# Loading shifted rows for a depthwise convolution by groups of channels to 128 partitions, adding its tiles by transfers, and reordering ScalarE's last instructions

## The chip, the core and the metric

The kernel runs on one core of a Trainium2 chip. The time is the device time of one execution, in microseconds (us). The kernel before takes 2873.85 us (median of three runs, 2868.29 to 2874.54).

## What is computed

Input x has shape [16, 384, 32, 32] in float32: 16 images, 384 channels, 1024 pixels each.

```python
# layer 0: group norm, attention over pixels (8 heads of 48), projection, residual
x = x + proj(softmax(q k^T * 48**-0.5) v)(_gn(x))
# layer 1: group norm, depthwise 7x7 convolution, residual
w_sym = (w + rot90(w, 1) + rot90(w, 2) + rot90(w, 3)) * 0.25
x = x + depthwise_conv(_gn(x), w_sym, padding=3)
```

The kernel exploits that w_sym is symmetric under rotation by 180 degrees only through sums and differences of columns; that part is not touched here.

## The kernel before

**Main body.** The channels lie on the 128 partitions, in three blocks k = 0, 1, 2. For each image b, TensorE makes q, k and v, then for each pair of heads the scores (L518) and the weighted sum (L538), then the projection (L599). ScalarE does the exponentials (L526). VectorE does the convolution of the image before: a tile (b, k) is one block of channels of one image. Its "folding" (fold_ops, L724) is a list of some 40 instructions: sums and differences of columns ("side", L733), multiply-adds into rows ("rows_e", "rows_o" and the output, L736), and adds of shifted rows (L746). ScalarE prepares it: fold_x writes the normalised tile with a margin ("padded", L704), and fold_first the first product of three rows_e tiles (L715). The finished tile is stored by conv_end (L821).

**The end.** Three tiles, PE_TILES = (14, 2), (15, 2) and (15, 1), are convolved by TensorE; of the last image VectorE folds only (15, 0). The route of a tile on TensorE is:

1. conv_begin normalises the tile and conv_store (L893) writes it to a DRAM buffer "xd": one channel takes 2 planes (rows of the image with even and with odd number) of PLANE = 19 rows of 32.
2. conv_load (L904) reads it back as "sh", one tile of 128 partitions by 4 groups by 512 for each half a of the channels. On the partitions lie 16 channels times RI = 8 shifts in the vertical; each of the 4 groups has another 16 channels. Before, there is one transfer for each shift i, to the 16 partitions from 16·i on, with 4 rows of 2 KB each: 8 transfers of 128 KB for a load. At the end (late["tail"]), odd i are issued by ScalarE's queue, the others by SP's.
3. conv_on_pe (L926) multiplies with banded matrices ("mat", made by conv_matrices from weights "wsh" and a stack of identities "eye"); a piece for one half has 28 matmuls: 7 horizontal taps times 4 groups. The tap dx is the outer loop, so the first 4 matmuls read all 4 groups.
4. conv_take (L953): ScalarE copies the half from PSUM to "rows". conv_perm (L958): TensorE sorts even and odd rows with a permutation into "ps_rows".
5. conv_add (L978): VectorE adds ps_rows to the residual x1 (L980), and a transfer stores the result (L981).

**What sets the order.** The schedule is written by hand: each engine runs its instructions in the order in which the Python program issues them. A planner estimates times: `clock` for TensorE, `vclock` for VectorE. `after(wait, cost, f)` queues a piece of VectorE work that becomes due `wait` us from now; `catch_up` issues due work first and otherwise the next instruction of the folding (`tap`); `applies` is a queue of ScalarE work. fast_end (L1461) issues the end of the last image: the statistics, the start of the convolutions, ScalarE's fold_x and fold_first, and the first permutation. The last loop of `run` issues the pieces on TensorE; between the first two pieces of (15, 2) on TensorE stands the matmul of the check of the softmax sums (check_tensor, L1373, L1376); it gives VectorE two tiny instructions (L1378, L1379), whose place on VectorE depends on what the planner has issued by then.

Transfers issued by SP or ScalarE use eight completion semaphores in turn; a transfer that takes one waits until the transfer that had it eight places before has landed. An engine that issues a transfer is held by that wait.

Of the kernel before, what the change touches and what calls it, by code (L numbers as in the profile page):

```python
# [10 lines left out]
F32 = mybir.dt.float32  # L11
I32 = mybir.dt.int32
AF = mybir.ActivationFunctionType
ALU = mybir.AluOpType
AX = mybir.AxisListType

P = 128
# [28 lines left out]
def kernel(  # L46
# [25 lines left out]
    nc = tc.nc  # L72

    B, C, H, W = x.shape
    N = H * W
# [4 lines left out]
    HALF = N // 2  # L80
# [39 lines left out]
    def run(general):  # L120
        tag = "g" if general else "f"
        with ExitStack() as stack:
# [14 lines left out]
            tpool = pool("tpool", 2)  # L137
# [6 lines left out]
            def psum(name):  # L144
                return ps_s.tile([P, 2, HALF], F32, tag="s", name=name)

            xns, x1s, qks, os_, accs, es, xn1s = {}, {}, {}, {}, {}, {}, {}
            xds, shs, pss, mats, psums = {}, {}, {}, {}, {}
# [32 lines left out]
            late, pps = {}, {}  # L181
# [18 lines left out]
            ident = wpool.tile([P, P], F32, name="ident")  # L200
# [13 lines left out]
            wsh = wpool.tile([P, 2, 8, 2, KS], F32, name="wsh")  # L214
# [446 lines left out]
            def by_rows(t):  # L661

                return t.rearrange("p (m q w) -> p q m w", q=2, w=W)

            def grids(t):
                return t.rearrange("p q (m w) -> p q m w", w=W)
# [153 lines left out]

            def conv_end(b, k):  # L821

                (nc.scalar if b == B - 1 and not general else nc.gpsimd).dma_start(  # L823
                    out[b, k * P : (k + 1) * P].rearrange("p h w -> p (h w)"), x1s.pop((b, k))
                )

# [5 lines left out]
            RI, CG = KS + 1, P // (KS + 1)  # L832
            NG = P // CG
            PLANE = (H // 2 + PAD) * W

            def conv_prepare():

                w_d = dconv.tile([C, (KS + 2) * KS], F32, tag="w", name="w_d")
                zero = tpool.tile([P, N], F32, tag="t", name="zero")[:, 0 : 2 * W]
                nc.gpsimd.memset(zero, 0.0)  # L840
                w_rows = w_d.rearrange("(k p) t -> p k t", p=P)
                with nc.allow_non_contiguous_dma(reason="small, once"):
                    nc.gpsimd.dma_start(
                        w_rows[:, :, KS : (KS + 1) * KS], wsym.rearrange("p k i j -> p k (i j)")
                    )
                    none = zero[:, 0 : NK * KS].rearrange("p (k t) -> p k t", k=NK)
                    nc.gpsimd.dma_start(w_rows[:, :, 0:KS], none)
                    nc.gpsimd.dma_start(w_rows[:, :, (KS + 1) * KS :], none)
                    for n, k in enumerate(PE_K):
                        for i in range(RI):  # L850
                            nc.gpsimd.dma_start(
                                wsh[CG * i : CG * (i + 1), n].rearrange("p g t d -> p g (t d)"),
                                bass.AP(
                                    w_d.tensor,
                                    w_d.offset + (k * P * (KS + 2) + i) * KS,
                                    [[(KS + 2) * KS, CG], [CG * (KS + 2) * KS, NG], [1, 2 * KS]],
                                ),
                            )
                for bk in PE_TILES:
                    xd = dconv.tile([P, 2 * PLANE], F32, tag=f"x_{len(xds)}", name=f"xd_{len(xds)}")  # L860
                    xds[bk] = xd

                    for lo, n in ((0, 1), (H // 2 + 1, 2), (H // 2 + 3, 2), (2 * PLANE // W - 1, 1)):
                        nc.gpsimd.dma_start(xd[:, lo * W : (lo + n) * W], zero[:, 0 : n * W])
                for q in range(RI):
                    src = ident[:, CG * q : CG * (q + 1)]
                    if q == 0:
                        nc.gpsimd.tensor_copy(eye, src)
                    else:
                        nc.gpsimd.tensor_tensor(eye, eye, src, ALU.add)  # L870
                for row in range(2):
                    nc.gpsimd.tensor_copy(
                        perm[:, row].rearrange("p (g c) -> p g c", c=CG),
                        ident.rearrange("p (g t c) -> p t g c", t=2, c=CG)[:, 1 - row],
                    )
# [28 lines left out]
            def conv_load(b, k, a):  # L904

                t = qkpool.tile([P, 2, N], F32, tag="qk", name=f"sh_{b}_{k}_{a}")
                t = t.rearrange("p a n -> p (a n)").rearrange("p (g n) -> p g n", n=HALF)
                xd = xds[b, k]
                for i in range(RI):
                    (nc.scalar if late.get("tail") and i % 2 else nc.sync).dma_start(  # L910
                        t[CG * i : CG * (i + 1)],
                        bass.AP(
                            xd.tensor,
                            xd.offset
                            + a * NG // 2 * CG * 2 * PLANE
                            + (0 if i % 2 else PLANE)
                            + i // 2 * W,
                            [[2 * PLANE, CG], [CG * 2 * PLANE, NG // 2], [1, HALF]],
                        ),
                    )  # L920
                shs[b, k, a] = t
# [29 lines left out]
            perms = deque()  # L951

            def conv_take(b, k, a):  # L953
                if a == 0 or (b, k) not in shs:
                    shs[b, k] = epool.tile([P, 2, HALF], F32, tag="e", name=f"rows_{b}_{k}")
                nc.scalar.copy(shs[b, k][:, a, :], pss.pop((b, k, a)))

            def conv_perm(b, k, a):  # L958

                nonlocal clock  # L960
                if (b, k) not in pss:
                    pss[b, k] = psum(f"ps_rows_{b}_{k}")
                part = slice(64 * a, 64 * a + 64)
                for row in range(2):
                    nc.tensor.matmul(
                        pss[b, k][part, row, :],
                        lhsT=perm[:, row],
                        rhs=shs[b, k][:, a, :],
                        start=True,
                        stop=True,  # L970
                    )
                clock += 2.2
                if (b, k) == PE_TILES[-1]:
                    after(0.5, 1.3, lambda: conv_add(b, k, part, (nc.scalar, nc.sync)[a]))
                elif a == 1:
                    after(3.5 if b < B - 1 else 0.5, 1.3, lambda: conv_add(b, k, slice(0, P), nc.gpsimd))

            def conv_add(b, k, part, queue):  # L978
                dst = by_rows(x1s[b, k][part])
                nc.vector.tensor_tensor(dst, grids(pss[b, k][part]), dst, ALU.add)  # L980
                queue.dma_start(  # L981
                    out[b, k * P + part.start : k * P + part.stop].rearrange("p h w -> p (h w)"),
                    x1s[b, k][part],
                )
# [89 lines left out]
            clock, vclock, catching = 0.0, 0.0, False  # L1074
# [10 lines left out]
            def after(wait, cost, f):  # L1085

                nonlocal count
                count += 1
                heapq.heappush(later, (now() + wait, count, cost, f))

            applies, count_a = [], 0
# [292 lines left out]
            def loads(n):  # L1384
                while n and pe_loads and pe_loads[0][0] in xn1s:
                    (b, k), a = pe_loads.popleft()
                    conv_load(b, k, a)
                    n -= 1
# [15 lines left out]
            def conv_rows():  # L1404
                for p in perms:
                    conv_take(*p)
                while perms:
                    conv_perm(*perms.popleft())
# [52 lines left out]
            def fast_end(b):  # L1461
                nonlocal clock, vclock
                assert not applies
                x1_stats[b].groups_on_pe(late["masks"], tap, lambda: conv_piece(False))
                conv_piece(False)
                x1_chains(b, x1_stats[b])
                clock = now()
                vclock = clock + 1.0
                after(0.0, 1.2, check_vector)
                heapq.heappop(applies)[-1]()  # L1470
                loads(2)
                clock += 3.0
                heapq.heappop(applies)[-1]()
                conv_rows()
                clock += 4.5

            def once(key, when):
                if when and key not in late:
# [4 lines left out]
            for b, n0, size in [  # L1483
# [31 lines left out]
                if b == B - 1:  # L1515
# [10 lines left out]
                    if once("ones", r >= 32):  # L1526
                        t = wv.rearrange("p k c -> p (k c)")[:, 0:N]
# [15 lines left out]
            while later or state["done"] < len(order) or active or pe_conv or perms:  # L1543
# [6 lines left out]
                else:  # L1550
                    clock = now() + 1.0
# [53 lines left out]
```

## Time and profile before

| | us |
|---|---|
| median of three runs | 2873.85 |
| the profiled execution | 2872.72 |
| its span (first to last instruction) | 2870.9 |
| TensorE busy | 2832.4 |
| VectorE busy | 2083.9 |
| ScalarE busy | 1649.1 |
| GpSimd (POOL) busy | 250.6 |
| last store issued | 2865.20 |

The granted TensorE clock is 0.994 of full speed. A line of a timeline gives start, length, engine, line of the source, operation, output <- inputs, and in brackets how long the engine stood idle before and who released it. SPq and ACTq are transfer issues on SP's and ScalarE's queues; the length there is the time over which a group of issues was spread. A "landing stamp" is an increment of the completion semaphore of a transfer, as the trace records it. TensorE's busy time is modelled; the last instruction of VectorE's folding ends at 2865.17.

### The profile page before, as it was taken

Reading aid. Unit: us, or ns where it says so; the run is one execution under the profiler, and the core shown is the slowest. Engines: PE = TensorE matmul, PEld = TensorE weight load, DVE = VectorE, ACT = ScalarE, POOL = GpSimd, SP = SyncE. Lnnn points to the kernel's source line nnn. Section 1 sums busy time; section 2 is a strip of 40 time slices with the busy share of each in tenths; the row PEclk is TensorE's granted clock in tenths of the full one; section 3 lists DMA queues with packets and bytes.
Section 4 is the critical chain, followed back from the end, with each engine's and each line's share of the span. In section 5 each row is a group of like instructions: output and inputs, shape, how many; then the busy total and the mean of one; then the engine's idle time right before and its main releaser. Section 6 shows DMA issues by size and latency. Waiting matters only on the chain.

```text
span 2870.9 us, 46047 instructions
## 1 busy us (share of the span) xinstructions
PE 2832.4 (99%) x19342; PEld 1115.2 (39%) x19342; DVE 2083.9 (73%) x2257; ACT 1649.1 (57%) x1925; POOL 250.6 (9%) x410
## 2 busy tenths in 40 slices
PE   9999999999999999999999999999999999999995
PEld 5344343433434344343433434344343433434331
DVE  4502968959597695968959597695968959597776
ACT  2637647475674747647475674747647375674730
POOL 3201012210101001010010101001010010101000
PEclk9999999999999999999999999999999999999998
DMA  6612131211212112130211212112130211212215
GB/s 239 189 37 49 32 75 29 53 49 44 63 33 62 45 37 64 32 75 24 50 50 44 63 33 62 45 37 63 32 75 24 50 50 44 64 33 60 78 39 103
DMA packets 75657, 167.35 MB, mean 58 GB/s; under 512 B 31952, under 2 KB 34000, under 8 KB 73904
## 3 DMA queue, kind: packets, MB, share of 16 engines
q0 software_dynamic: 32400, 107.53, 14.3%
q1 hardware_dynamic: 41536, 54.16, 7.5%
q10 hardware_dynamic: 1504, 2.62, 0.6%
q8 instruction: 154, 2.52, 0.4%
q14 instruction: 63, 0.52, 0.1%
HBM read 117.09 MB, written 28.68 MB: 51 GB/s over the span
## 4 chain that ended last, share of the span: by engine, by line
PE 95%; DVE 3%; DMA 1%; issue 1%; ACT 0%; ACTq 0%; POOL 0%; SPq 0%; DVEq 0%; POOLq 0%
PE ps_s L518 30%; PE acc L538 30%; PE ps_qk L447 17%; PE ps_v L473 9%; PE ps_proj L599 8%; DVE x L746 1%; DVE rows_e L736 1%; DMA sh<-xd 1%; PE warm L1325 0%; DVE side L733 0%; DMA inv<-rec 0%; DMA inv<-inv 0%; DVE rows_o L736 0%; DVE x L736 0%; DVE x L980 0%
## 5 line engine op out<-in xcount | busy, mean ns | idle before, releaser
L526 ACT ACTIVATE e<-ps_s 128x1024 f32<-128x1024 f32 x1024 | 1021.2, 1030 | 448.1 <-PE ps_s L518 447.4
L538 PE MATMUL acc<-e,v 64*64 64x512 f32 x8192 | 1040.5, 588 | 0.6 <-ACT o L551 0.6
L518 PE MATMUL ps_s<-qk 48*64 48x512 f32 x8192 | 1040.8, 589 | 0.0
L733 DVE TENSOR_TENSOR side<-padded 128x1024 f32<-128x1024 f32 x270 | 329.0, 1219 | 345.5 <-ACT padded L704 345.5
L736 DVE SCALAR_TENSOR_TENSOR rows_e<-side,even,rows_e 128x1024 f32<-128x1024 f32 x405 | 509.6, 1274 | 85.6 <-ACT rows_e L715 84.0
L538 PEld LDWEIGHTS acc<-e,v 64*64 64x64 f32 x8192 | 308.8, 132 | 575.8 <-issue 574.2
L518 PEld LDWEIGHTS ps_s<-qk 48*64 48x64 f32 x8192 | 307.5, 132 | 577.4 <-issue 525.8
L447 PE MATMUL ps_qk<-x,wqk 128*128 128x512 f32 x1152 | 502.8, 595 | 0.0
L447 PEld LDWEIGHTS ps_qk<-x,wqk 128*128 128x128 f32 x1152 | 218.2, 191 | 278.0 <-issue 272.4
L746 DVE TENSOR_TENSOR x<-x,rows_o 128x992 f32<-128x992 f32 (+3 forms) x271 | 309.8, 1144 | 3.0
L746 DVE TENSOR_TENSOR x<-x,rows_e 128x992 f32<-128x992 f32 (+2 forms) x270 | 310.8, 1151 | 0.0
L454 ACT COPY qk<-ps_qk 128x1024 f32<-128x1024 f32 x96 | 97.2, 1012 | 319.4 <-PE ps_qk L447 319.4
L473 PE MATMUL ps_v<-wv,x 128*128 128x384 f32 x768 | 252.6, 486 | 0.0
L599 PE MATMUL ps_proj<-o,wp 128*128 128x512 f32 x540 | 234.2, 592 | 0.0
L493 ACT COPY v<-ps_v 64x384 f32<-64x384 f32 x256 | 121.4, 474 | 122.5 <-PE ps_v L473 120.0
L473 PEld LDWEIGHTS ps_v<-wv,x 128*128 128x128 f32 x768 | 145.9, 190 | 108.2 <-issue 14.3
L736 DVE SCALAR_TENSOR_TENSOR rows_o<-side,odd,rows_o 128x1024 f32<-128x1024 f32 x135 | 172.8, 1280 | 1.6
L736 DVE SCALAR_TENSOR_TENSOR x<-side,even,x 128x1024 f32<-128x1024 f32 x135 | 172.5, 1278 | 0.0
L823 POOL DMA_DIRECT2D out<-x x44 | 24.8, 563 | 1600.3 <-DVE x L746 1599.8
L715 ACT ACTIVATE rows_e<-padded,even 128x1024 f32<-128x1024 f32 x135 | 146.7, 1166 | 11.0 <-DMA sh<-xd 11.0
L599 PEld LDWEIGHTS ps_proj<-o,wp 128*128 128x128 f32 x540 | 102.6, 190 | 126.2 <-issue 117.4
L607 ACT ACTIVATE x<-ps_proj,bp 128x1024 f32<-128x1024 f32 x45 | 50.1, 1114 | 167.6 <-PE ps_proj L599 167.6
(145 smaller groups left out, 1013.1 us busy)
## 6 DMA issues: line engine op xcount, KB each, us to landing
x<-in_x POOLq DMA_DIRECT2D x90, 512.0 KB, 5.5
inv<-inv SPq DMA_DIRECT2D x126, 256.0 KB
out<-x POOLq DMA_DIRECT2D x46, 512.0 KB, 3.0
xs<-in_x POOLq DMA_DIRECT2D x42, 512.0 KB, 6.4
qk<-qk POOLq DMA_DIRECT2D x96, 128.0 KB, 4.1
o<-o SPq DMA_DIRECT2D x180, 32.0 KB
sh<-xd SPq DMA_DIRECT2D x32, 128.0 KB
x<-in_x SPq DMA_DIRECT2D x6, 512.0 KB
```

The lines of the kernel that those rows point to most:

```text
L447: nc.tensor.matmul(ps[:, h, :], lhsT=wqk[:, k, s, t, :], rhs=xns[b][:, k, h * HALF : (h + 1) * HALF], start=(k == 0), stop=(k == NK - 1),)
L454: nc.scalar.copy(halves(qks[u][:, s, :]), ps)
L473: nc.tensor.matmul(ps[:, j, 0:C], lhsT=xns[b][:, k, t * P : (t + 1) * P], rhs=wv[:, k, :], start=(k == 0), stop=(k == NK - 1),)
L493: nc.scalar.copy(dst[:, :, 0 : HEADS // 2 * (D + 1)].rearrange("p k (h d) -> p k h d", d=D + 1)[:, :, :, 0:D], src.rearrange("p k (h d) -> ...
L518: nc.tensor.matmul(ps[64 * c : 64 * c + 64, a, :], lhsT=qk[r, 1, 64 * kb : 64 * kb + 64], rhs=qk[r, 0, h * HALF : (h + 1) * HALF], start=True,
L526: nc.scalar.activation(es[n], ps, AF.Exp, scale=SCALE)
L538: nc.tensor.matmul(accs[a][64 * j : 64 * j + 64, :], lhsT=v[rows, kb, c : c + 64], rhs=e[rows, j, :], start=(kb == 0), stop=(kb == 2 * NT ...
L599: nc.tensor.matmul(ps[:, h, :], lhsT=wp[:, t, o * P : (o + 1) * P], rhs=os_[b, t // 2][:, t % 2, h * HALF : (h + 1) * HALF], start=(t == 0 ...
L715: nc.scalar.activation(grid(rows_e[dy - 1]), padded_view(i), AF.Identity, scale=even[:, k, dy, 0:1],)
L733: vec.tensor_tensor(grid(sides[n]), padded_view(i, j), padded_view(i, -j), op)
L736: vec.scalar_tensor_tensor(dst, src, w, dst, ALU.mult, ALU.add)
L746: vec.tensor_tensor(dst, dst, src[:, lo + dy * W : hi + dy * W], op)
```

## The change

- conv_load issues 4 transfers of 256 KB for a load, one for each group of 16 channels, each to all 128 partitions, all on SP's queue. The partitions are now sorted by pair of shifts (4), then channel, then parity of the row, so that source and destination can be walked together: the source pattern is [W, 4], [PLANE, 32], [1, 512]. The new function `inputs(i)` gives the partitions of shift i, every second of 32; the weights and the stack of identities follow it.
- For (14, 2) and (15, 2), ScalarE copies ps_rows from PSUM to a tile "t", GpSimd's queue adds it to x1 by an accumulating transfer, and conv_end stores x1, on GpSimd's queue too. Before, VectorE added and GpSimd's queue stored. (15, 1) keeps VectorE's add, in two halves; its due time is 6.0 us after the permutation instead of 0.5.
- fast_end: ScalarE's copies of (14, 2) go ahead of fold_first, and the permutation goes behind it. The planner's clock grows by 3.0 at another place and no longer by 4.5 at the end.
- By the new clocks, the order on VectorE changes where the diff doesn't show it. The two reductions of the check (L1378, L1379 before) came after the first five instructions of the folding of (15, 0) and after the add of (14, 2); they now come before all of them. On TensorE the order is as before.

```diff
             def conv_end(b, k):

-                (nc.scalar if b == B - 1 and not general else nc.gpsimd).dma_start(
+                nc.gpsimd.dma_start(
                     out[b, k * P : (k + 1) * P].rearrange("p h w -> p (h w)"), x1s.pop((b, k))
                 )
...
+            def inputs(i):
+
+                first = i // 2 * 2 * CG + 1 - i % 2
+                return slice(first, first + 2 * CG - 1, 2)
...
-                                wsh[CG * i : CG * (i + 1), n].rearrange("p g t d -> p g (t d)"),
+                                wsh[inputs(i), n].rearrange("p g t d -> p g (t d)"),
...
-                    src = ident[:, CG * q : CG * (q + 1)]
+                    src = ident[:, inputs(q)]
...
-                for i in range(RI):
-                    (nc.scalar if late.get("tail") and i % 2 else nc.sync).dma_start(
-                        t[CG * i : CG * (i + 1)],
+
+                for i in range(NG // 2):
+                    nc.sync.dma_start(
+                        t[:, i],
                         bass.AP(
                             xd.tensor,
-                            xd.offset
-                            + a * NG // 2 * CG * 2 * PLANE
-                            + (0 if i % 2 else PLANE)
-                            + i // 2 * W,
-                            [[2 * PLANE, CG], [CG * 2 * PLANE, NG // 2], [1, HALF]],
+                            xd.offset + (a * NG // 2 + i) * CG * 2 * PLANE,
+                            [[W, RI // 2], [PLANE, 2 * CG], [1, HALF]],
                         ),
                     )
...
                 if (b, k) == PE_TILES[-1]:
-                    after(0.5, 1.3, lambda: conv_add(b, k, part, (nc.scalar, nc.sync)[a]))
+                    after(6.0, 1.3, lambda: conv_add(b, k, part, (nc.scalar, nc.sync)[a]))
                 elif a == 1:
-                    after(3.5 if b < B - 1 else 0.5, 1.3, lambda: conv_add(b, k, slice(0, P), nc.gpsimd))
+                    t = tpool.tile([P, N], F32, tag="t", name=f"conv_{b}_{k}")
+                    nc.scalar.copy(by_rows(t), grids(pss.pop((b, k))))
+                    nc.gpsimd.dma_start(x1s[b, k], t, accum_op=ALU.add)
+                    conv_end(b, k)
...
                 loads(2)
+                for p in perms:
+                    conv_take(*p)
+                heapq.heappop(applies)[-1]()
+                while perms:
+                    conv_perm(*perms.popleft())
                 clock += 3.0
-                heapq.heappop(applies)[-1]()
-                conv_rows()
-                clock += 4.5
```

## Prediction

> **What bounds the kernel now.** I read the table of slices first: TensorE is busy in every slice but the last, which reads 5. The body is therefore bound by TensorE's attention matmuls, and every line of the diff that runs more than once runs after 2700 us of the 2870.9 us span (the weight rows of conv_prepare run once, near 500 us, and are hidden). So only the last 170 us matter. Second I asked for the chain that ended last, from 2700 us on (start, length, what).
>
> ```profile
> 2798.11 2.83 DMA xd<-xn
> 2802.47 7.83 DMA sh<-xd
> 2810.69 3.23 ACT rows_e L715 x3
> 2814.53 4.08 PE ps_rows L965 x8
> 2818.63 1.23 DVE x L980
> 2819.86 1.13 DVE side L733
> ...
> 2843.51 1.13 DVE x L980
> ...
> 2853.25 1.23 DVE x L980
> ...
> 2863.98 1.20 DVE x L746 x2
> ```
>
> Read downwards: the normalised rows are stored, shifted rows are loaded, ScalarE gets to rows_e, TensorE permutes the tile (14,2), VectorE adds it, and from then on VectorE works without a gap to 2865.2. VectorE idled 19.5 us before 2818.63. Third, the timeline of the same stretch says why (start, length, engine or queue, line).
>
> ```profile
> 2801.09 22.32 SPq L910 DMA_DIRECT2D sh<-xd  x16
> 2801.12 9.52 ACTq L910 DMA_DIRECT2D sh<-xd  x8
> ...
> 2818.53 6.12 PE L941 MATMUL ps_conv<-sh,mat 128*32 128x512 f32 x56
> ...
> 2824.47 0.17 PE L1376 MATMUL ps_again<-lim,ones 128*1 128x2 f32 x1
> ...
> 2825.57 0.14 DVE L1378 TENSOR_REDUCE good<-ps_again 1x1 f32<-1x2 f32 x1
> ...
> 2849.26 1.93 PE L965 MATMUL ps_rows<-rows,perm 128*64 128x512 f32 x4 [0.70 <-ACT rows L956]
> ```
>
> Eight load issues in ScalarE's stream hold it for 9.5 us (each waits for the completion semaphore of an earlier transfer), so rows_e, the two copies and the permutation come late. VectorE's add L980 stands before its folding, so the folding waits too. Fourth, the windows give the loads' rate (us, PE, PEld, DVE, ACT, POOL busy; clock; DMA share; GB/s).
>
> ```profile
> 2799.00:2801.00 2.00, 1.05 (x12) 0.13 (x4) 0.12 (x2) 0.66 (x1) 0.00 (x0) 1.00 0.99 376
> 2819.00:2827.00 8.00, 7.33 (x74) 1.96 (x66) 7.97 (x9) 0.58 (x1) 0.59 (x1) 1.00 1.06 134
> ```
>
> The store to DRAM over 128 partitions moves 376 GB/s; the loads of 16 partitions each move about 131 (landing stamps: one transfer of 128 KB per 1.0 us from 2804.2 to 2835.5). All engines are equally full in both.
>
> [...] The new load's destination begins with 128 partitions, but its source begins with the 4 shifts ([W, 4], [PLANE, 32], [1, 512]), so **it would run on 4 engines**. The trace shows the rule at work once: sum<-o, whose sides both begin with 2, lands with three stamps (2711.57 at once, then 2712.25 and 2712.29), where the 16-partition loads land with sixteen. The forecast goes by this rule. I found no transfer in the trace whose two sides begin with unequal numbers.
>
> **The price of the load.** On one engine a 2 KB packet takes 82 ns at the least, and at 376 to 392 GB/s sixteen engines do 24 GB/s each. Four engines give at most 98 GB/s: 10.7 us for one load of 1 MB (four transfers). [...] I take the middle, **82 GB/s, 12.8 us**, against 8.0 us now, and keep both ends.
>
> **The sum, part by part**, against the profiled execution (2872.72 us; the median shown, 2873.85, lies 1.1 higher, and I add that at the end).
>
> 1. *ScalarE's end.* The 16 load issues leave its stream (15.3 us of it). After padded (2799.7) come the two copies (0.56, 0.58, once the convolution of (14,2) ends at 2800.05) and rows_e (3.2), done at 2804.5 instead of 2813.9; the permutation of (14,2) ends near 2805. What is late next: the order of VectorE's instructions has changed. The reduction L1378 now stands before all the folding. It waits for the matmul L1376, which TensorE reaches only after the first piece of (15,2), 6.1 us long, which waits for the first load. Behind it wait all of VectorE's folding and the two last adds.
> 2. *First load.* Data begin at 2802.7; 12.8 + 0.4 for landing gives 2815.9, the piece ends at 2822.0, and VectorE starts 1.3 later, at 2823.3 (in before, the reduction ran 0.9 behind its matmul and took 0.3 with the next). Its folding began at 2819.8 before.
> 3. *Adds by transfer.* VectorE loses two adds (1.23, 1.22); its work from start to end, 46.5 us, becomes 43.8 with the 0.25 of the check ahead of it. ScalarE gains two copies from PSUM of 128x1024 (1.01 each by L454), POOL two accumulating transfers (0.55 to issue; 5.5 to land by the x loads, 3.0 for the store behind). For (15,2) this ends by about 2859, before the end: hidden. The copy also stands before the copy of (15,1)'s first half, hidden while TensorE waits for the last load; with that cover gone it would cost up to 1 us of TensorE, not of VectorE.
> 4. *Last load.* Four loads in one queue end at 2802.7 + 51.2 + 0.4 = 2854.3. Then the first matmuls of the last piece 1.4 (of 1.85), permutation of the first half 2.0, rest of the piece 4.3, copy 0.65, second permutation 1.95 (the last row above), wake-up and add 1.5: 2866.1. Of VectorE's folding, 10.0 us stand behind this add (10.7 less one L739 that moves ahead). **End 2876.1 instead of 2865.2: +10.9.** VectorE alone would have been done at 2823.3 + 43.8 = 2867.1, so the load decides.
> 5. *Earlier loads, of (14,2).* They share SP's queue with the softmax sums. At 82 GB/s the first ends at 2730.8 (2728.8 now) and inv<-rec behind it as late; the second is issued after inv<-inv, ends at 2747.9, and sum<-o (two engines[...]) behind it. The reciprocal L568 would run at 2749.9 instead of 2748.2: +1.7, of which 0.3 to 0.6 is slack before TensorE's sums at 2774: **+1.4**. At 98 GB/s nothing, at 66 +7.4.
> 6. *Fewer issues on SP (24 less in all), the later due time of the last add (6.0 us), the new channel order, conv_end's queue:* nothing. SP has no other work there but the sums; the last add waits for TensorE anyway; the channel order changes which rows are taken, not how many.
>
> 2872.7 + 10.9 + 1.4 = 2885.0; with 1.1, **2886**. At 98 GB/s step 4 gives +2.5: 2876. At 66 it gives +23.3, with step 5 +30.7: 2904. Break-even is 104 GB/s.
>
> **Rivals.**
> - *All sixteen engines carry the load*[...]: 1 MB in 3.0 us at 350 GB/s. First load 2806.1, VectorE starts at 2813.5, needs 43.8, ends at 2857.3: -7.9; inv<-rec comes earlier, but only the 0.6 of slack before 2774 can be had. **2865, faster.** For it: 376 GB/s of the 128-partition store. Against: the rule and the three stamps. It decides from 104 GB/s upward.
> - *Four engines[...]:* 98 GB/s, **2876**, no change that can be measured. For it: many packets of inv<-inv, 64 partitions on 16 engines, take the minimum of 159 ns for 4 KB. Against: that is over within 16 KB an engine, and the second such transfer is slower.
> - *The rate stays at 131 GB/s* (the change doesn't widen the path): VectorE starts at 2818.5, ends at 2862.3: -2.9, **2871**, no change.
>
> **How the numbers follow.** About 0.2% (5.7 us) is what a measurement of this kernel can tell from no change. Four engines with conflicts: 0.60, 2886 (2880 to 2904). Four engines near their full rate: 0.15. Rate unchanged: 0.04. Sixteen engines: 0.21, 2865. Leaving the fast case out would leave out 0.21, so the range goes from 2863 to 2904. Faster 0.21, no change 0.19, slower 0.60.
>
> **What would show it.** A load landing with 5 stamps and not 16; transfers of 256 KB 2.7 to 4.0 us apart; DMA share near a quarter in the tail; rows_e near 2801 to 2805; L1378's counterpart on VectorE at about 2823 with no folding before it; VectorE idle before each add of (15,1); the last load landing near 2854. If loads land about 0.75 us apart and VectorE begins near 2813, the rule does not hold here and the kernel is faster.

## The result, and the profile after

The changed kernel takes 2886.25 us (median of five runs, 2885.32 to 2887.18), the kernel before 2873.37 us (five runs): a ratio of 1.0051, 95% interval 1.0036 to 1.0066. It is slower by half a per cent, clear of the noise. The forecast was 2886 us, slower. The profiled execution took 2886.04 us, its span 2884.3.

Up to about 2797 us the two kernels run alike, bound by TensorE; the loss lies behind that. The chain that ended last, in the changed kernel (start, length, what):

```profile
2797.40 2.84 DMA xd<-xn
...
2836.18 14.23 DMA sh<-xd
2850.46 1.83 PE ps_conv L944 x9
2852.28 1.86 PE ps_rows L968 x4
2854.14 4.24 PE ps_conv L944 x40
...
2859.04 1.95 PE ps_rows L968 x4
2861.01 1.22 DVE x L986
...
2867.08 1.24 DVE x L986
...
2877.14 1.19 DVE x L746 x2
```

Before, the chain left the loads at 2810.3, went over ScalarE's rows_e and TensorE's permutation, and was VectorE's own work from 2818.6 on. Now the loads hold it until 2850.5, then come the last piece, its permutation, and 17.3 us of VectorE. The timeline of the same stretch:

```profile
2800.14 2.33 PE L968 MATMUL ps_rows<-rows,perm 128*64 128x512 f32 x8 [0.80 <-ACT rows L959]
2800.32 38.42 SPq L916 DMA_DIRECT2D sh<-xd  x16
2800.36 3.25 ACT L715 ACTIVATE rows_e<-padded,even 128x1024 f32<-128x1024 f32 x3
...
2804.81 0.91 POOL L981 DMA_DIRECT2D x<-conv  x1 [8.48 <-ACT conv L980]
...
2814.20 0.55 POOL L823 DMA_DIRECT2D out<-x  x1 [8.48 <-DMA x<-conv]
2814.53 1.92 PE L944 MATMUL ps_conv<-sh,mat 128*32 128x512 f32 x2 [3.13 <-DMA sh<-xd]
2817.20 7.32 PE L944 MATMUL ps_conv<-sh,mat 128*32 128x512 f32 x48 [0.75 <-DMA sh<-xd]
...
2825.38 0.15 DVE L1384 TENSOR_REDUCE good<-ps_again 1x1 f32<-1x2 f32 x1 [26.97 <-PE ps_conv L944]
```

ScalarE is free at once (rows_e ends at 2803.6, before at 2813.9). But the check's reduction, first in VectorE's order, waits until 2825.4 for TensorE, and TensorE for the loads. (The profile counts 56 matmuls for a piece where the program issues 28.) VectorE's waits (total, times, longest):

```profile
DVE good L1384 <- PE ps_conv L944: 27.0, 1, 27.0
DVE x L986 <- PE ps_rows L968: 8.6, 1, 8.6
```

The windows of the load (the clock, the DMA share and GB/s are the last three columns):

```profile
2810.00:2814.00 4.00, 1.40 (x2) 0.00 (x0) 0.00 (x0) 0.00 (x0) 0.00 (x0) 0.50 0.26 69
...
2818.00:2822.00 4.00, 4.00 (x28) 1.53 (x24) 0.00 (x0) 0.00 (x0) 0.00 (x0) 0.54 0.26 101
...
2835.00:2840.00 5.00, 5.00 (x50) 1.44 (x47) 4.96 (x6) 0.58 (x1) 0.00 (x0) 1.00 0.26 98
```

The DMA share is a quarter (0.26): as much as four of sixteen engines, and 98 GB/s. Each transfer lands with five stamps, one at once and four together; a later one has 2826.13, 2826.19, 2826.30 and 2826.37, the next 2.7 us later. A packet of 2 KB takes 87 ns (median), where the loads of before took 236 on one queue and 244 on the other.

### The profile page after: what moved, and what is told of

It is laid out like the page before. It is cut to its first block, busy times and chain, and to the rows that moved or that the text cites. A ratio compares the mean times of both kernels' runs of the same rounds, so it can differ in the third digit from the quotient of the medians.

```text
span 2884.3 us, 45997 instructions
## 1 busy us (share of the span) xinstructions
PE 2843.2 (99%) x19342; PEld 1123.7 (39%) x19342; DVE 2081.3 (72%) x2255; ACT 1650.7 (57%) x1927; POOL 253.3 (9%) x412
```

## Experiments

**How the runs are compared.** Whole runs of one kernel spread by some 8 to 12 us (before: 2868.6 to 2877.1 in thirty runs, 2867.8 to 2879.4 in thirteen others). In the traces, the attention part is alike to a few hundredths, but sits up to 3.4 us earlier or 0.8 later than in the trace of before, by differences in the first 280 us; and in five traces TensorE's clock dropped near 2792, in four for 3.4 us and in one for 10.2 us (windows there show 0.50 to 0.82), which put the tail about 1.6 to 2.3 us later (ScalarE's wait for the statistics is 8.8 or 9.5 us in these and 7.2 in the others). So beside the medians I use the **tail**: from the start of xn's normalisation on VectorE (L363 in the changed kernel, 2796.56 there, 2797.27 before) to the end of the span. "Folding from" and "last load" count from the same point, all three in us.

| kernel | median us | ratio to before, 95% | tail | folding from | last load |
|---|---|---|---|---|---|
| before | 2872.4 to 2874.4 | | 73.7 | 22.5 | 38 |
| changed | 2886.25 | 1.0051 (1.0036 to 1.0066) | 87.7 | 29.1 | 54 |
| dimensions exchanged | 2867.07 | 0.9979 (0.9972 to 0.9986) | 66.7 | 16.8 | 22 |
| late adds | 2878.61 | 1.0025 (1.0012 to 1.0038) | 79.4 | 28.9 | 54 |
| no accumulating transfer | 2883.89 | 1.0040 (1.0026 to 1.0054) | 83.4 | 25.5 | 50 |
| before, new loads | 2878.87 | 1.0021 (1.0010 to 1.0032) | 79.7 | 9.8 | 51 |
| before, all loads on SP | 2867.55 | 0.9975 (0.9965 to 0.9985) | 67.1 | 9.8 | 33 |
| early check | 2881.35 | 1.0024 (1.0014 to 1.0034) | 82.1 | 6.3 | 54 |
| early check, late adds | 2874.03 | 1.0002 (0.9993 to 1.0011) | 74.5 | 6.3 | 54 |
| due time put back | 2886.43 | 1.0044 (1.0028 to 1.0061) | 86.6 | 28.9 | 54 |
| halved transfers | 2957.45 | 1.0289 (1.0272 to 1.0306) | 135.8 | 40 | 99 |
| all three repaired | 2858.70 | 0.9945 (0.9929 to 0.9962) | 56.9 | 6.3 | 22 |

### The dimensions of the source exchanged

```diff
-                first = i // 2 * 2 * CG + 1 - i % 2
-                return slice(first, first + 2 * CG - 1, 2)
+                first = i // 2 + RI // 2 * (1 - i % 2)
+                return slice(first, first + RI * (CG - 1) + 1, RI)
...
-                            [[W, RI // 2], [PLANE, 2 * CG], [1, HALF]],
+                            [[PLANE, 2 * CG], [W, RI // 2], [1, HALF]],
```

> The changed kernel with one edit: the two outer dimensions of the load's source change places (channel planes first, shifts second), and the partitions are numbered to match. Bytes, packets, queue, number of transfers and every instruction on the engines stay. Theory A (the outermost dimension of the source, 4, limits the load to 4 engines): landing stamps become 16 or so, 256 KB about 0.75 us apart instead of 2.65, the first four have landed near 2806, VectorE starts near 2813 instead of 2825.4, and the kernel takes about 2865 us. Rival (the load is slow because its rows overlap in DRAM, or because of its bytes, whatever the order): still 2.65 us per 256 KB and 2886 us.

Measured: 2867.07 us. Every transfer lands with sixteen stamps. From 2816.6 to 2820.6 the transfers of 256 KB end 0.63 to 0.69 us apart; before that, while GpSimd's accumulating transfer is under way (it lands at 2816.35), 0.6 to 2.4 us apart. A window, and two lines of the timeline of this kernel:

```profile
2814.00:2820.00 6.00, 5.33 (x36) 1.50 (x28) 4.01 (x6) 0.58 (x1) 0.55 (x1) 1.00 1.04 371
```

```profile
2803.19 12.41 SPq L916 DMA_DIRECT2D sh<-xd  x16
...
2815.95 0.15 DVE L1384 TENSOR_REDUCE good<-ps_again 1x1 f32<-1x2 f32 x1 [14.67 <-PE ps_conv L944]
```

The core's transfers run at 371 GB/s instead of 98, with a DMA share of 1.04 instead of 0.26 (GpSimd's two transfers have a part in this window; by the landings just named, the loads alone reach some 390). The bytes and packets of the loads are the same. The order of two dimensions decided here; the rival (bytes, overlapping rows) falls. VectorE folds from 16.8 instead of 29.1, and then needs the 44 us that the forecast gave it. The change as it stands loses 21.0 us of tail by this alone, and would have been faster than before without it.

### A dose: two engines

```diff
-                for i in range(NG // 2):
+                for i, j in [(i, j) for i in range(NG // 2) for j in range(2)]:
                     nc.sync.dma_start(
-                        t[:, i],
+                        t[P // 2 * j : P // 2 * (j + 1), i],
...
-                            xd.offset + (a * NG // 2 + i) * CG * 2 * PLANE,
-                            [[W, RI // 2], [PLANE, 2 * CG], [1, HALF]],
+                            xd.offset + (a * NG // 2 + i) * CG * 2 * PLANE + 2 * j * W,
+                            [[W, RI // 4], [PLANE, 2 * CG], [1, HALF]],
```

> A dose: the changed kernel with each load transfer cut in two, one for each two pairs of shifts, to 64 partitions each, so that the source begins with a dimension of 2 instead of 4. Theory A (the outermost dimension of the source sets the number of engines): 3 stamps for each transfer, 2 engines, 128 KB per 2.7 us, that is 49 GB/s; 16 transfers for one tile pair of loads more, the last load lands some 40 us later (near 2890), and the kernel takes 2920 to 2930 us. Rival 1 (the number of engines goes by partitions or by packets of a transfer): 5 stamps or more and 2886 us or a little more. Rival 2 (two transfers in a row take different engines): 98 GB/s and 2886 us.

Measured: 2957.45 us. A window and a wait of this kernel:

```profile
2840.00:2860.00 20.00, 10.50 (x58) 2.50 (x56) 1.35 (x3) 0.00 (x0) 0.00 (x0) 0.64 0.13 49
```

```profile
PE ps_proj_last L643 <- DVE o L580: 19.5, 1, 19.5
```

Three stamps each, 128 KB per 2.7 us, 49 GB/s, a DMA share of an eighth (0.13): as theory A says for an outermost dimension of 2. The time I had forecast was some 30 us too low. The wait shows most of that: the earlier loads, those of (14,2), share SP's queue with the softmax sums, and at 49 GB/s TensorE stood still for 19.5 us before L643. That is the forecast's step 5, which I left out of this expectation. The table has most of the rest: the last load lands 45 us later than in the changed kernel where I had said 40, and 37 us stand behind it instead of 34.

### The adds of (15,1): late, and as before

Late adds:

```diff
-                    after(6.0, 1.3, lambda: conv_add(b, k, part, (nc.scalar, nc.sync)[a]))
+                    after(40.0, 1.3, lambda: conv_add(b, k, part, (nc.scalar, nc.sync)[a]))
```

> The changed kernel with the due time of the two adds of (15,1) at 40 us instead of 6, so that they come behind nearly all of VectorE's folding. Theory (VectorE's 8.6 us of idle before the first of these adds lie on the path that sets the end): the folding behind them fills that idle time, the last add still waits for TensorE (second permutation 2861.0), and the end moves from 2878.3 to about 2870: 2878 us, -8.5. Rival (the order on VectorE makes no difference, since the last load sets the end): 2886 us.

Measured: 2878.61 us, tail -8.3. The timeline of VectorE shows both adds at the very end, without a wait:

```profile
2863.40 3.54 DVE L746 TENSOR_TENSOR x<-x,rows_o 128x960 f32<-128x960 f32 x4
2866.86 2.47 DVE L986 TENSOR_TENSOR x<-ps_rows,x 64x1024 f32<-64x1024 f32 x2
```

The 8.6 us of idle time lay on the path. Due time put back:

```diff
-                    after(6.0, 1.3, lambda: conv_add(b, k, part, (nc.scalar, nc.sync)[a]))
+                    after(0.5, 1.3, lambda: conv_add(b, k, part, (nc.scalar, nc.sync)[a]))
```

> The changed kernel with the due time of the two adds of (15,1) put back to 0.5 us. The first add then stands six instructions earlier on VectorE, and before the second one. Theory A (an add of the first half waits wherever it stands, since the load is late): VectorE reaches it near 2847 and waits for the first permutation (near 2854.2), folds 5.6 us, and takes the second add right behind the second permutation at 2861; 16 us follow as before, end near 2877.2 instead of 2878.3: 2885 us, -1. Rival (the later due time by itself carries the 8.6 us of idle time): -6 to -8, 2878 to 2880 us.

Measured: 2886.43 us, tail -1.1. VectorE's two adds in this kernel:

```profile
2852.22 1.22 DVE L986 TENSOR_TENSOR x<-ps_rows,x 64x1024 f32<-64x1024 f32 x1 [7.56 <-PE ps_rows L968]
...
2859.05 1.23 DVE L986 TENSOR_TENSOR x<-ps_rows,x 64x1024 f32<-64x1024 f32 x1
```

The idle time only moved forward to the first add. The second add now stands where the first stood in the changed kernel, and starts at the same moment (2859.05; this trace lies 2.0 us earlier, and there it was 2861.01). Behind that moment there is one add less, 16.1 us of work instead of 17.3. So the later due time by itself costs 1.1 us. What matters is how much of the folding stands behind the adds when the load comes so late.

### The accumulating transfer and store of (14,2) left out

```diff
-                    nc.gpsimd.dma_start(x1s[b, k], t, accum_op=ALU.add)
-                    conv_end(b, k)
+                    if b == B - 1:
+                        nc.gpsimd.dma_start(x1s[b, k], t, accum_op=ALU.add)
+                        conv_end(b, k)
```

> The changed kernel without the accumulating transfer and the store of tile (14,2): that tile is left out of the output, ScalarE's copy of it stays. Theory (the accumulating transfer and the store take turns with the loads on the four engines that carry them, and cost the first load some 5 us): transfers of the first load land 2.65 us apart without the gap, the last of the four near 2812.5 instead of 2817.2, all later ones as much earlier, and the kernel takes about 2881 us, -4.5 to -5. Rival (the gap has another cause, such as the waits for completion semaphores on SP's queue): gap and time stay, 2886 us.

Measured: the four transfers of the first load let TensorE go on at even distances (timeline of TensorE):

```profile
2808.08 1.04 PE L944 MATMUL ps_conv<-sh,mat 128*32 128x512 f32 x2 [3.54 <-DMA sh<-xd]
2810.76 1.91 PE L944 MATMUL ps_conv<-sh,mat 128*32 128x512 f32 x2 [1.63 <-DMA sh<-xd]
2813.44 1.92 PE L944 MATMUL ps_conv<-sh,mat 128*32 128x512 f32 x2 [0.77 <-DMA sh<-xd]
2816.11 6.87 PE L944 MATMUL ps_conv<-sh,mat 128*32 128x512 f32 x48 [0.75 <-DMA sh<-xd]
```

In the changed kernel they start at 2805.72, 2809.49, 2814.53 and 2817.20. The gaps of 3.8 and 5.0 us are gone, the last load lands 4.3 us earlier after xn, the tail is 4.3 us shorter. The medians alone could not show this: 2883.89 against 2886.25, and the intervals of the ratios overlap. In the changed kernel the transfer's stamps show the same from the other side: twelve at 2809.3 to 2809.6, four only at 2813.7 to 2813.9.

### The kernel before with the new loads alone

```diff
-                for i in range(RI):
-                    (nc.scalar if late.get("tail") and i % 2 else nc.sync).dma_start(
-                        t[CG * i : CG * (i + 1)],
+                for i in range(NG // 2):
+                    nc.sync.dma_start(
+                        t[:, i],
```

With it go the source's pattern, `inputs` and its two uses, as in the change; the adds and fast_end stay as before.

> The kernel before with the new loads alone (four engines, all on SP's queue, partitions renumbered); adds, their due times and the order on ScalarE and VectorE stay. Theory (the loads' rate costs, and the freed ScalarE gives back): ScalarE is done with its rows near 2804, VectorE folds from about 2808 on, the last load lands near 2846 to 2850, the last permutation ends near 2857 to 2861 and what stands behind the last add follows: 2874 to 2880 us, slower than before by 1 to 7. Rival (the new loads cost nothing, the loss comes from the adds' new order): 2866 us or less, since VectorE would start 10 us earlier.

Measured: 2878.87 us, tail +6.0 against before. VectorE in this kernel:

```profile
2806.18 1.22 DVE L733 TENSOR_TENSOR side<-padded 128x1024 f32<-128x1024 f32 x1
...
2824.40 0.15 DVE L1380 TENSOR_REDUCE good<-ps_again 1x1 f32<-1x2 f32 x1 [12.34 <-PE ps_conv L943]
...
2858.42 1.23 DVE L982 TENSOR_TENSOR x<-ps_rows,x 64x1024 f32<-64x1024 f32 x1 [0.32 <-PE ps_rows L967]
```

VectorE starts 12.7 us earlier than before, then waits for the check and for the late load. So the loads alone make the kernel slower; the rest of the change adds 8.0 us of tail.

### The kernel before with all its loads on SP's queue

```diff
-                    (nc.scalar if late.get("tail") and i % 2 else nc.sync).dma_start(
+                    nc.sync.dma_start(
```

> The kernel before with one edit: all its loads of 16 partitions go to SP's queue, none to ScalarE's. Theory (the issues in ScalarE's stream hold rows_e and the permutation, and with them VectorE): rows_e done near 2804 instead of 2813.9, VectorE's first add near 2806 instead of 2818.6, the loads still one 128 KB transfer per 1.0 us and the last near 2835.5, the end near 2857: 2864 to 2867 us. Rival (the loads keep VectorE back, not the issues): the end stays near 2865 and the time near 2872.

Measured: 2867.55 us, tail -6.5. Timeline and a window of this kernel:

```profile
2803.77 23.93 SPq L910 DMA_DIRECT2D sh<-xd  x32
2805.58 1.05 ACT L956 COPY rows<-ps_conv 128x512 f32<-128x512 f32 x2
...
2808.65 1.22 DVE L980 TENSOR_TENSOR x<-ps_rows,x 128x1024 f32<-128x1024 f32 x1 [6.78 <-PE ps_rows L965]
...
2821.49 0.15 DVE L1378 TENSOR_REDUCE good<-ps_again 1x1 f32<-1x2 f32 x1 [5.82 <-PE ps_again L1376]
```

```profile
2819.00:2827.00 8.00, 7.25 (x58) 2.09 (x54) 5.44 (x7) 0.59 (x1) 0.00 (x0) 1.00 1.07 176
```

Taking the issues off ScalarE lets VectorE fold 12.7 us earlier; the check takes 5.8 of it back. What I had wrong: the loads are also faster on one queue, 176 GB/s here where two queues gave 127 to 135 in windows from 2810 to 2826, and the last lands 5 us earlier. So this run does not say how the 6.5 us divide between the freed ScalarE and the faster loads. The earlier start of VectorE, though, comes from ScalarE: the add L980 waits for the permutation alone.

### The check ahead of the first piece

```diff
             fast_end(B - 1)
+            catch_up(clock)
+            check_tensor(lims.pop())
             while later or state["done"] < len(order) or active or pe_conv or perms:
                 if pe_conv:
-                    if pe_conv[0][0] == B - 1 and lims:
-                        check_tensor(lims.pop())
```

> The changed kernel with the check of the softmax sums ahead of the first piece of (15,2), due time 6.0 us as it is. Theory (the last load decides, VectorE's start doesn't): VectorE folds from about 2803.5 instead of 2825.4, but then waits for the second permutation at 2861 and has 12 us of folding behind it, where the planner now puts two instructions more ahead of the adds: end near 2873.5 instead of 2878.3: 2881 us, -4 to -5. Rival (VectorE's late start by itself is the loss): -15 or more, 2871 us.

Measured: 2881.35 us, tail -5.6. With the late adds as well:

> The changed kernel, loads still on four engines, with two edits in VectorE's order: the check of the softmax sums ahead of the first piece of (15,2) on TensorE, and the two adds of (15,1) last. Theory (the slow load costs only through what VectorE waits for): VectorE folds from about 2803.5 without a gap and is done before the second permutation ends at 2861; the two adds follow, end near 2863.5 instead of 2878.3: 2871 us, about the kernel before. Rival (VectorE's order is not what carries the loss): nothing beyond the 8 us of the run with the late adds alone, 2878 us.

Measured: 2874.03 us, tail -13.2. The wait for the second permutation in the first and in the second of these kernels:

```profile
2863.20 1.22 DVE L986 TENSOR_TENSOR x<-ps_rows,x 64x1024 f32<-64x1024 f32 x1 [25.52 <-PE ps_rows L968]
```

```profile
2863.96 2.48 DVE L986 TENSOR_TENSOR x<-ps_rows,x 64x1024 f32<-64x1024 f32 x2 [16.73 <-PE ps_rows L968]
```

VectorE gains 22.8 us at its start in both, but an earlier start alone only lengthens the wait for the last load, and 11.4 us of VectorE's work still stand behind it (the two adds and 8.9 us of folding). With the adds last, nothing but them is left behind that wait, and the kernel is as fast as before (1.0002) with loads that land 16 us later. The slow load costs through what waits for it and what stands behind that.

### All three repaired

The exchanged dimensions, the early check and the late adds together.

> The changed kernel with the source's dimensions exchanged (16 engines) and both edits of VectorE's order (check ahead of the first piece, adds last). Theory: with the loads done near 2822 and the second permutation near 2842, nothing but VectorE's own 44 us of work is left; it starts near 2806 instead of 2816 of the run with the exchanged dimensions alone, and the time is about 2857 us, some 16 below the kernel before. Rival (something else ends the run by then, such as the stores): 2860 to 2867 us.

Measured: 2858.70 us, 0.9945 of before (0.9929 to 0.9962). VectorE:

```profile
2803.84 1.21 DVE L733 TENSOR_TENSOR side<-padded 128x1024 f32<-128x1024 f32 x1
...
2845.27 2.47 DVE L986 TENSOR_TENSOR x<-ps_rows,x 64x1024 f32<-64x1024 f32 x2
```

From 2803.8 to 2847.7 VectorE has no gap: 43.9 us, its own work. This version beats both kernels. By this trace the next bound is how early VectorE may start; no run tried that.

## Why the prediction held, and which terms were off

1. **Four engines: right.** The forecast went by the number with which the two sides of a transfer begin. The trace of before showed that for equal numbers alone (sum<-o, 2 and 2, three stamps; the loads, 16 and 16, sixteen). The changed kernel (source 4, destination 128: five stamps, DMA share 0.26, 98 GB/s), the exchange (32 and 128: sixteen stamps, 1.04, 371 GB/s) and the dose (2 and 64: three stamps, 0.13, 49 GB/s) agree with it, also where the two sides begin with unequal numbers, which the trace of before did not show. No run varied the outermost dimension of the destination by itself.
2. **The price of the load: the term was off.** I took 82 GB/s, the middle between 98 and 66. The 98 was worked out from the trace of before, a quarter of the 392 GB/s that all sixteen engines moved there; the 66, half of the 131 GB/s of the loads of before, was my estimate for engines that hold each other up. No run shows such a conflict: the changed kernel's loads ran at 98 GB/s and 87 ns a packet where nothing else ran on these engines (windows from 2822 to 2826 and from 2835 to 2848), the upper end. Of the rivals, as to the rate, it was the one with four engines at 98 GB/s that came true. Yet the mean over the four loads is about 12 us each and not 10.7, since the transfers of (14,2) share the engines: 4.3 us by the run that left them out. So two errors partly met: four loads at 98 GB/s take 8.4 us less than at 82, and half of it was lost again. The last load landed at 2850.4, not 2854.3.
3. **ScalarE's end: right.** rows_e done at 2803.6 (forecast 2804.5) and the permutation at 2802.5 (near 2805); the check's reduction is what is late next (2825.4, forecast 2823.3). The delay there has two parts of some 1.2 us each: the first load was there for TensorE at 2817.2 and not at 2815.9, and what was left of the first piece then took 7.3 us, where I had taken 6.1 for the whole. TensorE's clock stood at 0.50 to 0.54 of full speed up to 2821.7, after its waits (windows above).
4. **The tail behind the last load: the term that was furthest off.** The way from the landing to the end of the second permutation took 10.6 us (forecast 10.3). Behind it I had counted 11.5 us: wake-up, the second add and 10.0 us of folding. It took 17.3 us, because the *first* add waited for the second permutation too, and it and 4.9 us of folding stand ahead of the second. That add is the first half's (its store leaves on ScalarE's queue), and its own permutation was done at 2854.1. With the due time put back it started right behind its own permutation; so the later due time, which in the program's order puts it behind the second permutation, is the likely cause of that wait, though no run varied this alone. In step 6 I had called the order there free ("the last add waits for TensorE anyway"). Putting the due time back gains only 1.1 us, but moving both adds back gains 8.3: the place of the adds was not free. VectorE idle before *each* add was among my signs; it idled before the first alone.
5. **Adds by transfer: hidden behind VectorE's work, but not free for the loads.** Step 3 looked at what comes behind the transfer of (15,2), which is hidden as I said. That the transfer of (14,2) would slow the loads I did not weigh.
6. **The earlier loads: +1.4 forecast, nothing measured.** At 98 GB/s the forecast itself gave nothing. The reciprocal L568 was late all the same, at 2750.07 (forecast 2749.9, before 2748.20), and no run shows why at this rate. It did not get through: the last division L580 ran only 0.6 us later than before (2756.45, 2755.86), and TensorE's matmuls L643, which need it, started 0.96 us earlier (2756.40, 2757.36), the lead that the attention part has in this trace. At two engines (the dose) the same delay did cost: 19.5 us before L643.

Summed from before's own frame: the last load 5.3 us earlier than forecast with step 5, the piece and its permutations 0.3 longer, VectorE behind them 5.8 longer: 0.8 later in all. That the total came so near is luck: the errors cancel.

The sign was in part luck too. With the rate that came, 98 GB/s, the forecast's own sum says 2876 us, no change that can be measured. What lies between that and 2886 are two terms that it put at nothing: the transfers of (14,2) among the loads (the last load 4.5 us later than at 98 GB/s throughout) and the first add's place behind the second permutation (5.8 us). What does not depend on luck is shown by the exchanged dimensions: four engines instead of sixteen, and a last load so late that VectorE waits for it.

## What to carry to other kernels

Before a DMA is widened to more partitions, look at the outermost dimension of its *source* too: exchanging two dimensions of the source here was worth 19 us (2886.25 to 2867.07), with the same bytes and packets. Count the landing stamps and read the DMA share in a window: here five stamps and 0.26 went with 98 GB/s, three and 0.13 with 49, sixteen and 1.04 with 371. When a transfer becomes late, look through each in-order engine for the instruction that waits for it first and for the work queued behind it: repairing the two such waits here gained 6 and 8 us, together 13 of the 14 us of tail that were lost, with the load as slow as ever.

## What the runs showed of the hardware

- TensorE's clock fell in its waits for the loads: the windows of the changed kernel show 0.50 from 2806 to 2818, and the piece behind them was slower (7.32 us for 48 of its 56 records); with the exchanged dimensions the windows from 2802 to 2834 show 1.00 throughout. The matmuls of a piece took 7.8 us after a wait of 5.0 us in the kernel before with all loads on SP (clock 0.63 from 2813 to 2819), and 5.9 us at full clock (here in the kernel with the exchanged dimensions):

```profile
2813.58 7.80 PE L941 MATMUL ps_conv<-sh,mat 128*32 128x512 f32 x56 [4.96 <-DMA sh<-xd]
```

```profile
2824.13 5.88 PE L944 MATMUL ps_conv<-sh,wqk 128*32 128x512 f32 x56
```

So the slow load cost twice here. The clock stood at half speed for 13.7 us in before (2805.4 to 2819.0), and for 17.1 us (2804.6 to 2821.7) and 3.4 us (2828.5 to 2831.9) in the changed kernel. The runs do not show how long TensorE has to stand still for that: the clock fell 5.3 us after the last matmul in before (at 2805.4, idle from 2800.05), 2.2 us after it in the changed kernel (at 2804.6, idle from 2802.47) and 2.0 us after it with all loads on SP (at 2810.64, idle from 2808.62), and in the five traces with a drop near 2792 TensorE was idle for 0.80 us in all from 2788 to 2796.
- GpSimd's accumulating transfer, with sixteen stamps, ended with the slowest of them: while the loads ran at a DMA share of 0.26, twelve stamps came at 2809.3 to 2809.6 and the last four at 2813.7 to 2813.9, and the store behind it, issued at 2814.20, waited for those.
- Loads to 16 partitions each ran faster on one queue than on two. With the odd shifts on a second queue, transfers of 128 KB landed 0.86 us apart up to 2811 and 1.0 us apart from there to 2827; on one queue 0.94 us apart up to 2816 and 0.75 us apart from 2819 to 2830. No run here tells why.
